# Layer 0 of a two-layer graph network: where the adjacency bits come from, when score pieces are filled, and which engines split q and k

## The chip, the cores and the metric

One core of a Trainium2 chip runs the whole program. The metric is the device time of one execution in microseconds, as the median over several runs. The engines are TensorE (PE, matrix products into PSUM), VectorE (DVE), ScalarE (ACT), GpSimd (POOL) and SyncE (SP), which here only issues DMA transfers. Each engine works through its own queue in order. [...]

## The reference

3327 rows of 128 features, an adjacency matrix of zeros and ones, and two layers. Layer 0 is cosine attention over the neighbours with a residual and a layer norm. Layer 1 is eight-head attention whose q, k and v are reshaped in an unusual way, with the adjacency added twice to the scores.

```python
def _L0_gnn_ref(x, adj, beta):
    norm2 = jnp.linalg.norm(x, axis=1, keepdims=True)
    cos = beta[0] * (x @ x.T) / (norm2 @ norm2.T + 1e-07)
    masked = cos + (1.0 - adj) * -1000000000.0
    P = jax.nn.softmax(masked, axis=1)
    return P @ x

def _L1_gnn_ref(x, spatial_encoding, edge_encoding, Wq, Wk, Wv, Wo):
    ...
    q = (x @ Wq.T).reshape(d, n, h)
    k = (x @ Wk.T).reshape(d, n, h)
    v = (x @ Wv.T).reshape(d, n, h)
    a = jnp.einsum('dnh,dmh->dnm', q, k) * scale
    a = a + spatial_encoding + edge_encoding
    a = jax.nn.softmax(a, axis=2)
    out = jnp.einsum('dnm,dmh->dnh', a, v)
    out = out.reshape(n, h * d)
    return out @ Wo.T

x = _layernorm(x + _L0_gnn_ref(x, adj, L0_gnn_beta), axis=-1)
x = _layernorm(x + _L1_gnn_ref(x, adj, adj, Wq, Wk, Wv, Wo), axis=-1)
```

## The kernel before

The rows are cut into 26 tiles of 128 (N = 3327 is padded to 3328). Layer 0 is a software pipeline written out by hand: the outer loop `for t in range(-2, T + 3)` makes one round for each tile, and the inner loop takes eight steps `k`. In one round the stages of five tiles are interleaved:

- tile t+3: `load` fetches the adjacency rows as fp32 (the buffer `raw`, which shows as `kn` in the profile; three such buffers), at step 5. `load_bits` fetches the same rows for tile t+4 once more through POOL's queue, converted to bf16 on the way (`bits`, two buffers).
- tile t+2: `adj_chunk` multiplies strided columns of `bits` by a unit matrix on PE (L396), which turns them, and ACT copies them as bf16 to `aT` (L397, one buffer); after seven chunks `aT` is written to DRAM for layer 1 (L399).
- tile t+1: the inverse of the norm products, by a logarithm and exponentials on ACT (L410, L417) and Newton steps on DVE (L424, L431), and `mask`, which turns `raw` into an additive mask in place (L403).
- tile t: `scores`. Four pieces of 832 columns; for each, `score_piece` makes two fp32 products on PE (L359) into a two-bank buffer `sc` (two buffers), and DVE scales (L441) and masks them and takes the running minimum (L444).
- tile t-1: `weights` (the exponentials, L460), `turn_weights` (transposes on PE, L134, copied to SBUF by DVE or ACT, L474 and L472) and `weigh0` (the product with x, L482).
- tile t-2: the layer norm (`norm_begin`, `norm_root`, `norm_end`) and `project_turn`, the transposed x1.
- tile t-3: `project`. Six products of 512 columns (L533) with the three weight matrices into the PSUM tile `pq`, which has one buffer: k = 0 and 1 make q, 2 and 3 make k, 4 and 5 make v. For q and k, ACT copies the product to SBUF (`row`, L549; q with its scale), POOL rounds it to `high` (L554) and subtracts to get `low` (L555), and SP writes both to DRAM (L558). For v, ACT copies to `nine` (L535) and SP writes it (L539).

Within one engine the order is the order of the code (a manual schedule for PE, ACT, DVE and POOL); the order on SP is chosen by a scheduler. In rounds from tile 8 on, `gather` rearranges q and k in DRAM for layer 1; its transfers have no fixed place on SP's queue and appear in many rounds.

Rounds 26 to 28 have no new tile. They finish the last three tiles while `first_max` already searches the maxima for layer 1, using the same `sc` buffers.

Layer 1 follows and takes the rest of the time. Its per-step order on PE, ACT, DVE and POOL is written out as well.

Of the kernel before, what the change touches and what calls it, by code (L numbers as in the profile page):

```python
# [45 lines left out]
def gnn_two_layers(  # L46
# [297 lines left out]
    with ExitStack() as l0:  # L344
        big = l0.enter_context(tc.tile_pool(name="l0_big", bufs=1))
        adj_raw = l0.enter_context(tc.tile_pool(name="adj_raw", bufs=2))
# [21 lines left out]
        tiles = [Tile0() for _ in range(T)]  # L368
        half = NP // 2
# [12 lines left out]
        def load_bits(t: int):  # L382

            u = tiles[t]
            u.bits = adj_raw.tile([P, NP], BF16, name="bits", bufs=2)
            load_adj(u.bits, nc.gpsimd, t)

        def adj_chunk(t: int, c: int):

            u = tiles[t]  # L390
            if c == 0:
                u.aT = ptp.tile([P, T, P], BF16, name="aT", bufs=1)
            a, b = 4 * c, min(4 * c + 4, T)
            tp = ps_tp.tile([P, 4, P], F32, name="tp")
            for k in range(a, b):
                nc.tensor.matmul(tp[:, k - a], every(u.bits, k), unit, start=True, stop=True)  # L396
            nc.scalar.copy(u.aT[:, a:b, :], tp[:, : b - a])  # L397
            if c == NCH - 1:
                nc.sync.dma_start(aT_s[t], u.aT.rearrange("p t k -> p (t k)"))  # L399
# [34 lines left out]

        def scores(t: int, j: int):
            u = tiles[t]
            if j == 0:
                u.s = work.tile([P, NP], F32, name="s")
                u.mn = small.tile([P, NPC], F32, name="mn")
            sc = score_piece(xT[:, t * P : (t + 1) * P], xT, j)  # L440
            nc.vector.scalar_tensor_tensor(  # L441
                piece(u.s, j), sc, by_q[:, t : t + 1], piece(u.y, j), op0=ALU.mult, op1=ALU.mult
            )
            nc.vector.tensor_tensor_reduce(  # L444
                out=piece(u.s, j),
                in0=piece(u.s, j),
                in1=piece(u.raw, j),
                scale=-1.0,
                scalar=BIG if j == 0 else u.mn[:, j - 1 : j],
                op0=ALU.add,  # L450
                op1=ALU.min,
                accum_out=u.mn[:, j : j + 1],
            )
# [73 lines left out]
        def project(t: int, k: int):  # L527
# [5 lines left out]
            nc.tensor.matmul(pq, u.x1T, ws[n][:, cols], start=True, stop=True)  # L533
            if n == 2:
                nc.scalar.copy(  # L535
                    nine[:, i * 64 : (i + 1) * 64, :H], pq.rearrange("p (s h) -> p s h", h=H)
                )
                if i == 1:
                    nc.sync.dma_start(  # L539
                        bass.AP(  # L540
                            tensor=v_s.tensor,
                            offset=v_s.offset + t * P * P * R9,
                            ap=[[P * R9, P], [1, P * R9]],
                        ),
                        nine.rearrange("p s r -> p (s r)"),
                    )
                return
            row = ptp.tile([P, 512], F32, name="row", bufs=2)
            nc.scalar.activation(  # L549
                row, pq, AF.Copy, scale=float(D) ** -0.5 if n == 0 else 1.0  # L550
            )
            high = ptp.tile([P, 512], F32R, name="high")
            low = ptp.tile([P, 512], F32R, name="low")
            nc.gpsimd.tensor_copy(high, row)  # L554
            nc.gpsimd.tensor_tensor(low, row, high.bitcast(F32), ALU.subtract)  # L555
            dst = (qn_s, kn_s)[n]
            for c, part in enumerate((high, low)):
# [9 lines left out]
        with tc.manual_schedule(  # L567
# [23 lines left out]
            for t in range(2):  # L591
                load_bits(t)
            nine = big.tile([P, P, R9], F32, name="nine")
            nc.gpsimd.memset(nine[:, :, H], 1.0)
# [31 lines left out]
            for i in range(2):  # L626
                nc.gpsimd.tensor_copy(
                    ws[i].rearrange("p (h s) -> p h s", h=H),
                    given[i].rearrange("p (s h) -> p h s", h=H),
                )  # L630

            k_first = 0
            for t in range(-2, T + 3):

                def there(n: int):
                    return 0 <= n < T

                for k in range(8):
                    if k == 0:
                        if there(t - 1):  # L640
                            weights(t - 1, 0)
                        if there(t - 3):
# [3 lines left out]
                        if there(t):  # L646
                            scores(t, 0)
# [3 lines left out]
                        if there(t - 3):  # L651
                            project(t - 3, 1)
                        if there(t - 2):
                            norm_root(t - 2)
                        if t >= T:
                            first_max(k_first)
                            k_first += 1
                        continue
                    if there(t) and k < NPC:
                        scores(t, k)  # L660
# [16 lines left out]
                    if k < 5 and there(t - 3):  # L677
                        project(t - 3, k + 1)
                    if k == 5 and there(t - 2):
                        project_turn(t - 2)  # L680
                    if there(t + 2):
# [14 lines left out]
                if there(t + 4) and t + 4 > 1:  # L696
                    load_bits(t + 4)
# [347 lines left out]
```

## Time and profile before

| what | value |
| --- | --- |
| median of 3 runs | 15358.9 us (15358.85 to 15360.56) |
| profiled execution | 15361.3 us, span 15359.5 us |
| PE, DVE, ACT, POOL busy over the span | 99%, 90%, 83%, 90% |
| granted TensorE clock, mean | 0.995 |
| start of layer 0 until the regular rounds | 0 to 121.8 us |
| regular rounds of tiles 3 to 23 | 121.8 to 668.9 us |
| rounds of tiles 24 and 25, drain, hand-over to layer 1 | 668.9 to 831 us |

How to read the lines shown further on. A row of the view by stretches gives the stretch, its length, then for PE, PE's weight loads, DVE, ACT and POOL the busy time with the number of instructions, then the granted clock, the mean busy share of the DMA engines and GB/s. A row of the timeline gives the start, the length, the engine, the line, the operation, the tiles written and read, the shapes and the count; in square brackets stands how long the engine was idle before it and what released it. A row of the waits gives who waited for whom, the total in us, the number of times and the longest. A matmul in fp32 shows as two records.

### The profile page before, as it was taken

Reading aid. Unit: us, or ns where it says so; the run is one execution under the profiler, and the core shown is the slowest. Engines: PE = TensorE matmul, PEld = TensorE weight load, DVE = VectorE, ACT = ScalarE, POOL = GpSimd, SP = SyncE. Lnnn points to the kernel's source line nnn. Section 1 sums busy time; section 2 is a strip of 40 time slices with the busy share of each in tenths; the row PEclk is TensorE's granted clock in tenths of the full one; section 3 lists DMA queues with packets and bytes.
Section 4 is the critical chain, followed back from the end, with each engine's and each line's share of the span. In section 5 each row is a group of like instructions: output and inputs, shape, how many; then the busy total and the mean of one; then the engine's idle time right before and its main releaser. Section 6 shows DMA issues by size and latency. Waiting matters only on the chain.

```text
span 15359.5 us, 494776 instructions
## 1 busy us (share of the span) xinstructions
PE 15192.6 (99%) x210460; PEld 6695.5 (44%) x210460; DVE 13818.7 (90%) x15851; ACT 12755.2 (83%) x25413; POOL 13765.0 (90%) x8979
## 2 busy tenths in 40 slices
PE   8899999999999999999999999999999999999999
PEld 5534444444444444444444444444444444444555
DVE  7889999999999999999999999999999999998776
ACT  7689998888888888888888888888888888888777
POOL 3389999999999999999999999999999999998887
PEclk9999999999999999999999999999999999999999
DMA  7732221111111111111111111111111111111112
GB/s 229 226 103 97 101 98 60 48 51 48 56 50 47 52 53 53 46 53 46 60 47 53 47 58 48 51 48 55 51 46 53 46 59 46 53 46 62 62 59 83
DMA packets 553135, 1018.81 MB, mean 66 GB/s; under 512 B 148711, under 2 KB 493284, under 8 KB 504582
## 3 DMA queue, kind: packets, MB, share of 16 engines
q1 hardware_dynamic: 547126, 965.00, 19.1%
q0 software_dynamic: 3792, 22.15, 0.8%
q8 instruction: 1648, 27.00, 0.7%
q14 instruction: 569, 4.66, 0.1%
HBM read 871.04 MB, written 192.54 MB: 69 GB/s over the span
## 4 chain that ended last, share of the span: by engine, by line
PE 96%; DMA 1%; DVE 1%; ACT 1%; issue 0%; SPq 0%; POOL 0%; DVEq 0%; ACTq 0%; POOLq 0%
PE acc L808 30%; PE ea L778 22%; PE m L262 16%; PE eb L791 13%; PE ea L791 10%; PE ea L797 1%; PE ea L764 1%; DMA aT_s<-aT 1%; PE eb L797 1%; PE acc L482 0%; PE pq L533 0%; PE sc L359 0%; ACT aT L397 0%; PE pp L993 0%; DMA qn_s<-high 0%
## 5 line engine op out<-in xcount | busy, mean ns | idle before, releaser
L899 POOL TENSOR_TENSOR pb<-pb,eT 128x768 f32<-128x768 f32 (+1 forms) x7488 | 13175.3, 1767 | 980.4 <-ACT pb L898 594.0
L277 DVE TENSOR_REDUCE mx<-m 128x2 f32<-128x1024 f32 x6753 | 8275.0, 1225 | 958.6 <-PE eb L797 555.4
L898 ACT ACTIVATE pb<-eb 128x768 f32<-128x768 f32 (+1 forms) x7488 | 5898.0, 788 | 2255.7 <-PE eb L797 1731.1
L262 PE MATMUL m<-kn,qx 32*128 32x512 f32 (+1 forms) x23128 | 6804.0, 471 | 0.1
L922 ACT ACTIVATE pa<-ea 128x384 f32<-128x384 f32 (+1 forms) x14976 | 6338.9, 478 | 23.0 <-PE ea L778 8.4
L808 PE MATMUL acc<-pb,vt 128*9 128x384 f32 (+1 forms) x29952 | 5903.7, 474 | 0.1
L808 PE MATMUL acc<-pa,vt 128*9 128x384 f32 (+1 forms) x29952 | 5903.7, 474 | 0.0
L298 DVE TENSOR_REDUCE mx<-m 128x1 f32<-128x512 f32 x6371 | 4338.5, 681 | 252.0 <-PE m L262 232.3
L791 PEld LDWEIGHTS <-one 3*128 3x128 bf16 x29952 | 1465.8, 91 | 5659.0 <-issue 4661.4
L778 PE MATMUL ea<-aT,two 128*32 128x384 bf16 (+1 forms) x59904 | 3715.6, 325 | 0.0
L797 PE MATMUL eb<-qx,kn 32*128 32x384 f32 (+1 forms) x13312 | 3030.2, 451 | 0.0
L797 PE MATMUL ea<-qx,kn 32*128 32x384 f32 (+1 forms) x13312 | 2938.7, 433 | 0.0
L262 PEld LDWEIGHTS m<-kn,qx 32*128 32x128 f32 x23128 | 2797.6, 182 | 216.3 <-DVE mx L298 4.7
L791 PE MATMUL ea<-cx,one 3*128 3x384 bf16 (+1 forms) x14976 | 2724.4, 324 | 0.2
L791 PE MATMUL eb<-cx,one 3*128 3x384 bf16 (+1 forms) x14976 | 2466.1, 326 | 16.9 <-ACT cx L869 16.7
L808 PEld LDWEIGHTS acc<-pa,vt 128*9 128x9 f32 x29952 | 1418.2, 91 | 399.9
L808 PEld LDWEIGHTS acc<-pb,vt 128*9 128x9 f32 x29952 | 1418.6, 91 | 387.0 <-issue 0.7
L778 PEld LDWEIGHTS <-two 128*32 128x32 bf16 x59904 | 938.1, 94 | 1421.5 <-issue 1231.0
L797 PEld LDWEIGHTS eb<-qx,kn 32*128 32x128 f32 x13312 | 1275.0, 188 | 0.0
L797 PEld LDWEIGHTS ea<-qx,kn 32*128 32x128 f32 x13312 | 1237.0, 182 | 8.0 <-issue 1.3
L302 DVE TENSOR_REDUCE mx<-m 128x2 f32<-128x512 f32 x1084 | 739.7, 682 | 20.3 <-PE m L262 19.1
L554 POOL CAST high<-row 128x512 fp32r<-128x512 f32 x104 | 96.0, 923 | 328.7 <-DMA qn_s<-high 209.9
(134 smaller groups left out, 5972.2 us busy)
## 6 DMA issues: line engine op xcount, KB each, us to landing
kn<-kp_s SPq DMA_DIRECT2D x512, 832.0 KB
vt<-v_s SPq DMA_DIRECT2D x288, 409.5 KB
kn<-kq_s SPq DMA_DIRECT2D x64, 832.0 KB
qx<-qp_s SPq DMA_DIRECT2D x1016, 48.0 KB
kn<-in_adj_dram SPq DMA_DIRECT2D x25, 1663.5 KB
qp_s<-qn_s SPq DMA_DIRECT2D x64, 416.0 KB
kp_s<-kx SPq DMA_DIRECT2D x32, 832.0 KB
kq_s<-kn_s SPq DMA_DIRECT2D x64, 415.9 KB
```

What stands on the lines that cost most here:

```text
L262: nc.tensor.matmul(dst, u.qx[rows(a), q * P : (q + 1) * P], u.km[rows(a), k0:k1], start=True, stop=True,)
L277: nc.vector.tensor_reduce(u.mx[:, h, qs[0], c], m, axis=AX.X, op=ALU.max)
L298: nc.vector.tensor_reduce(u.mx[:, a, qs[0], c : c + 1], m, axis=AX.X, op=ALU.max)
L302: nc.vector.tensor_reduce(u.mx[:, a, qs[0] : qs[1] + 1, c], m.rearrange("p (q k) -> p q k", q=2), axis=AX.X, op=ALU.max,)
L764: nc.tensor.matmul(dst[r], parts[u.i % 2][:, q, h], unit, start=start, stop=True, tile_position=(0, 32 * h), skip_group_check=True,)
L778: nc.tensor.matmul(e[r, : u.nq], two[:, r], aT[:, j, : u.nq], start=False, stop=True, tile_position=(0, 32 * c), skip_group_check=True,)
L791: nc.tensor.matmul(e[:, : u.nq], one[r], u.cx[r, : u.nq], start=True, stop=False, skip_group_check=True)
L797: nc.tensor.matmul(e[:, : u.nq], u.kx[rows(a), j * P : (j + 1) * P], u.qx[rows(a), : u.nq], start=False, stop=stop, skip_group_check=True,)
L808: nc.tensor.matmul(acc[32 * h : 32 * h + H + 1, : u.nq], u.vt[:, h, j], pts[h][:, : u.nq], start=(j == 0), stop=(j == T - 1), tile_positio ...
L898: nc.scalar.activation(pt_b[:, :, : u.nq], e_b[:, :, : u.nq], AF.Exp)
L899: nc.gpsimd.tensor_tensor(pt_b[:, :, : u.nq], pt_b[:, :, : u.nq], eT[:, j, : u.nq].unsqueeze(1).to_broadcast([P, 2, u.nq]), ALU.mult,)
L922: nc.scalar.activation(pt_a[:, h, : u.nq], e[:, : u.nq], AF.Exp)
```

## The change

Layer 1 isn't touched. In layer 0:

1. `load_bits` and its buffers go. `adj_chunk` reads the upper 16 bits of each fp32 word of `raw` as bf16 (`upper`), before `mask` overwrites `raw`. `aT` gets two buffers.
2. The score product leaves `scores` and becomes `fill`. The pieces 2 and 3 of tile t are filled at the ends of steps 0 and 1, the pieces 0 and 1 of tile t+1 at the ends of steps 6 and 7 of the round before.
3. `project` no longer makes `row`. ACT copies `pq` to `high`; in `project_rest` PE adds `less` (minus the unit matrix) times `high` to `pq` in PSUM, and ACT copies the remainder to `low`. POOL has no part in it. The scale of q moves into the weights, once at the start. `project` moves from the end of a step to the start of the next, and `project_turn` from step 5 to step 6. `nine` gets two buffers.

```diff
-        def load_bits(t: int):
...
+        def upper(t: int, k: int):
+
+            halves = tiles[t].raw.bitcast(BF16)
+            return halves.rearrange("r (p t h) -> r t h p", t=T, h=2)[:, k, 1, :]
...
-                u.aT = ptp.tile([P, T, P], BF16, name="aT", bufs=1)
+                u.aT = ptp.tile([P, T, P], BF16, name="aT", bufs=2)
...
-                nc.tensor.matmul(tp[:, k - a], every(u.bits, k), unit, start=True, stop=True)
+                nc.tensor.matmul(tp[:, k - a], upper(t, k), unit, start=True, stop=True)
...
+        def fill(t: int, j: int):
+            if there(t):
+                tiles[t].sc[j] = score_piece(xT[:, t * P : (t + 1) * P], xT, j)
...
-            sc = score_piece(xT[:, t * P : (t + 1) * P], xT, j)
+            sc = u.sc.pop(j)
...
-            nc.tensor.matmul(pq, u.x1T, ws[n][:, cols], start=True, stop=True)
+            nc.tensor.matmul(pq, u.x1T, ws[n][:, cols], start=True, stop=n == 2, skip_group_check=True)
...
-            row = ptp.tile([P, 512], F32, name="row", bufs=2)
-            nc.scalar.activation(
-                row, pq, AF.Copy, scale=float(D) ** -0.5 if n == 0 else 1.0
-            )
-            high = ptp.tile([P, 512], F32R, name="high")
+            u.pq = pq
+            u.high = ptp.tile([P, 512], F32R, name="high")
+            nc.scalar.copy(u.high, pq)
+
+        def project_rest(t: int, k: int):
+
+            u = tiles[t]
+            n, i = divmod(k, 2)
             low = ptp.tile([P, 512], F32R, name="low")
-            nc.gpsimd.tensor_copy(high, row)
-            nc.gpsimd.tensor_tensor(low, row, high.bitcast(F32), ALU.subtract)
+            nc.tensor.matmul(
+                u.pq, less, u.high, start=False, stop=True, skip_group_check=True
+            )
+            nc.scalar.copy(low, u.pq)
...
-            nine = big.tile([P, P, R9], F32, name="nine")
-            nc.gpsimd.memset(nine[:, :, H], 1.0)
+            nines = [big.tile([P, P, R9], F32, name=f"nine{i}") for i in range(2)]
...
-            for i in range(2):
-                nc.gpsimd.tensor_copy(
+            for i, by in enumerate((float(D) ** -0.5, 1.0)):
+                nc.gpsimd.tensor_scalar(
...
+            less = big.tile([P, P], F32R, name="less")
+            nc.vector.tensor_scalar_mul(less, ident, -1.0)
...
                     if k == 0:
                         if there(t - 1):
                             weights(t - 1, 0)
+                        if there(t):
+                            scores(t, 0)
                         if there(t - 3):
                             project(t - 3, 0)
                         if there(t - 2):
                             norm_begin(t - 2)
-                        if there(t):
-                            scores(t, 0)
                         if there(t - 1):
                             turn_weights(t - 1, 0)
                             weights(t - 1, 1)
-                        if there(t - 3):
-                            project(t - 3, 1)
                         if there(t - 2):
                             norm_root(t - 2)
+                        fill(t, 2)
+                        if there(t - 3):
+                            project_rest(t - 3, 0)
...
+                    if there(t - 3) and k < 6:
+                        project(t - 3, k)
...
-                    if k < 5 and there(t - 3):
-                        project(t - 3, k + 1)
-                    if k == 5 and there(t - 2):
+                    if k == 1:
+                        fill(t, 3)
+                    if k < 4 and there(t - 3):
+                        project_rest(t - 3, k)
+                    if k == 6 and there(t - 2):
                         project_turn(t - 2)
+                    if k >= 6:
+                        fill(t + 1, k - 6)
...
-                if there(t + 4) and t + 4 > 1:
-                    load_bits(t + 4)
```

More of the change, by code (lines that the diff above doesn't have):

```diff
@@ L345, in gnn_two_layers @@
         big = l0.enter_context(tc.tile_pool(name="l0_big", bufs=1))
-        adj_raw = l0.enter_context(tc.tile_pool(name="adj_raw", bufs=2))
         work = l0.enter_context(tc.tile_pool(name="l0_work", bufs=2))
@@ L368, in gnn_two_layers, with there @@
         tiles = [Tile0() for _ in range(T)]
+        for u in tiles:
+            u.sc = {}
+        def there(n: int):
+            return 0 <= n < T
         half = NP // 2
@@ L380, in load @@
                 nc.sync.dma_start(u.xr[:LAST], rows_of(x, t, D, LAST))
-        def load_bits(t: int):
-            u = tiles[t]
-            u.bits = adj_raw.tile([P, NP], BF16, name="bits", bufs=2)
-            load_adj(u.bits, nc.gpsimd, t)
+        def upper(t: int, k: int):
+            halves = tiles[t].raw.bitcast(BF16)
+            return halves.rearrange("r (p t h) -> r t h p", t=T, h=2)[:, k, 1, :]
         def adj_chunk(t: int, c: int):
@@ L532, in project @@
             pq = ps_x.tile([P, 512], F32, name="pq")
-            nc.tensor.matmul(pq, u.x1T, ws[n][:, cols], start=True, stop=True)
+            nc.tensor.matmul(pq, u.x1T, ws[n][:, cols], start=True, stop=n == 2, skip_group_check=True)
             if n == 2:
+                nine = nines[t % 2]
                 nc.scalar.copy(
@@ L547, in project @@
                 return
-            row = ptp.tile([P, 512], F32, name="row", bufs=2)
-            nc.scalar.activation(
-                row, pq, AF.Copy, scale=float(D) ** -0.5 if n == 0 else 1.0
-            )
-            high = ptp.tile([P, 512], F32R, name="high")
-            low = ptp.tile([P, 512], F32R, name="low")
-            nc.gpsimd.tensor_copy(high, row)
-            nc.gpsimd.tensor_tensor(low, row, high.bitcast(F32), ALU.subtract)
+            u.pq = pq
[4 more added lines that the diff above has]
+            n, i = divmod(k, 2)
+            low = ptp.tile([P, 512], F32R, name="low")
+            nc.tensor.matmul(
+                u.pq, less, u.high, start=False, stop=True, skip_group_check=True
+            )
+            nc.scalar.copy(low, u.pq)
             dst = (qn_s, kn_s)[n]
-            for c, part in enumerate((high, low)):
+            for c, part in enumerate((u.high, low)):
                 nc.sync.dma_start(
@@ L590, in gnn_two_layers @@
                 load(t)
-            for t in range(2):
-                load_bits(t)
-            nine = big.tile([P, P, R9], F32, name="nine")
-            nc.gpsimd.memset(nine[:, :, H], 1.0)
+            nines = [big.tile([P, P, R9], F32, name=f"nine{i}") for i in range(2)]
+            for nine in nines:
+                nc.gpsimd.memset(nine[:, :, H], 1.0)
             given = one_n.tile([P, NP], F32, name="n")
@@ L625, in gnn_two_layers @@
             nc.scalar.preload_act_table_set("natural_log_exp_and_others")
-            for i in range(2):
-                nc.gpsimd.tensor_copy(
+            for i, by in enumerate((float(D) ** -0.5, 1.0)):
+                nc.gpsimd.tensor_scalar(
                     ws[i].rearrange("p (h s) -> p h s", h=H),
                     given[i].rearrange("p (s h) -> p h s", h=H),
-                )
+                    by,
+                    None,
+                    op0=ALU.mult,
+                )
+            less = big.tile([P, P], F32R, name="less")
+            nc.vector.tensor_scalar_mul(less, ident, -1.0)
             k_first = 0
             for t in range(-2, T + 3):
-                def there(n: int):
-                    return 0 <= n < T
                 for k in range(8):
```

## The prediction

> **What bounds the kernel now.** The diff touches the first layer only, so I read the busy times by stretch first, to see how much of the span that is and which engine is full there. The twenty-one regular rounds (one row tile each, from tile 3 to tile 23) fill 121.8 to 668.9 us; what follows up to 831 us is the drain.
>
> ```profile
> 147.20:172.30 25.10, 22.76 (x135) 15.87 (x134) 23.11 (x32) 20.57 (x27) 9.40 (x11) 1.00 0.85 251
> 506.00:536.20 30.20, 25.03 (x135) 16.84 (x134) 21.28 (x29) 20.56 (x28) 14.08 (x14) 0.89 0.81 246
> 121.80:668.90 547.10, 494.08 (x2795) 343.62 (x2794) 468.40 (x653) 426.89 (x548) 222.41 (x228) 0.97 0.82 245
> ```
>
> The columns are length, then busy time of PE, weight loads, DVE, ACT and POOL, then granted clock, DMA share and GB/s. The first row is a clean round: 25.1 us, with PE at 22.8, DVE at 23.1, ACT at 20.6 and the DMA engines at 85%. The second is a round that lost 5 us to transfers, with no more work on any engine. The third gives the mean, 547.1 / 21 = 26.05 us, so about one microsecond of each round is transfer trouble (21 x 0.95 = 20 us in all). The other 14.5 ms run the same code before and after.
>
> No engine is full, so the round is set by waits. The waits of the same stretch, and ACT's instructions in the clean round in order of time:
>
> ```profile
> DVE s L441 <- PE sc L359: 50.6, 38, 6.8
> ACT row L549 <- PE pq L533: 35.9, 36, 1.6
> ACT nine L535 <- PE pq L533: 27.0, 20, 1.6
> ACT aT L397 <- PE tp L396: 20.2, 23, 1.8
> ```
> ```profile
> 147.25 1.70 ACT L460 ACTIVATE s<-s,mn 128x1664 f32<-128x1664 f32 x1
> 148.83 0.20 ACT L460 ACTIVATION_READ_ACCUMULATOR s<-s,mn 128x1 f32 x1
> 148.92 0.60 ACT L549 ACTIVATE row<-pq 128x512 f32<-128x512 f32 x1
> 149.40 1.69 ACT L460 ACTIVATE s<-s,mn 128x1664 f32<-128x1664 f32 x1
> ...
> 151.06 0.60 ACT L549 ACTIVATE row<-pq 128x512 f32<-128x512 f32 x1
> ...
> 151.90 3.06 ACT L410 ACTIVATE y<-norm_k,norm_c 128x3328 f32<-128x3328 f32 x1
> 155.21 0.60 ACT L549 ACTIVATE row<-pq 128x512 f32<-128x512 f32 x1 [0.26 <-PE pq L533]
> 155.70 1.59 ACT L417 ACTIVATE y<-y 128x1664 f32<-128x1664 f32 x1
> 158.80 0.60 ACT L549 ACTIVATE row<-pq 128x512 f32<-128x512 f32 x1 [1.51 <-PE pq L533]
> 159.29 1.58 ACT L417 ACTIVATE y<-y 128x1664 f32<-128x1664 f32 x1
> 162.33 0.59 ACT L535 COPY nine<-pq 128x512 f32<-128x512 f32 x1 [1.45 <-PE pq L533]
> 162.81 3.07 ACT L403 ACTIVATE kn<-kn,minus 128x3328 f32<-128x3328 f32 x1
> ```
>
> The reader is to see two things. From the first exponential (147.25) to the first copy of v (162.33) is 15.1 us, and the rest of the round, up to the next exponential at 172.34, is 10.0. And between any two reads of the bank pq (L549, L549, L549, L549, L535) stands an exponential, a logarithm or another long function: while ACT does that, PE fills pq again, so ACT hardly waits (3.2 us in the round, all because PE's steps are full: scores, turn, weighing and projection from 154.95 to 158.54 and again to 162.13 are 3.59 us without a gap).
>
> **The split of q and k: this sets the forecast.** pq has one buffer. Before, row frees it and POOL splits off the path. After, pq(k) is read by ACT (high), reduced by PE (minus high), and read by ACT again (low); only then may PE write pq(k+1). In the changed kernel's order low(k) is followed on ACT at once by high(k+1) (after k=3 by the first copy of v), with nothing between them. So four times a round ACT waits for a projection that can't start before ACT's own last instruction ends. The drain of the trace before has just that pair, two rows with nothing between:
>
> ```profile
> 739.31 0.60 ACT L549 ACTIVATE row<-pq 128x512 f32<-128x512 f32 x1 [4.50 <-PE pq L533]
> 741.18 0.60 ACT L549 ACTIVATE row<-pq 128x512 f32<-128x512 f32 x1 [1.27 <-PE pq L533]
> ```
>
> 1.27 us idle at full clock. ACT's pace, start to start: exponential 1.67, copy of 512 columns 0.48, logarithm 3.05, each L417 1.57, the two small ones 0.36 together. First part of the round: exponentials 3.34, high 4 x 0.48 = 1.92, low 4 x 0.48 = 1.92, small 0.36, logarithm 3.05, L417 3.14: 13.73. Waits 4 x 1.27 = 5.08. Sum 18.8 us against 15.1: +3.7 a round.
>
> Is the subtraction itself late? It isn't in the trace; the nearest row, the 128x512 fp32r product of L262, took 0.50 us alone, and three on different rows of the array started within 0.01 us, so 0.17 to 0.50; as a plain fp32 product it would be L533's 0.86. For k=2 and 3 it follows turn 0.43 and weighing 0.90, and low stands behind L417 1.57: 1.33 + 0.50 is just hidden, at 0.86 it costs 0.2. For k=1 a logarithm covers it. For k=0 PE has turn, a score piece of 1.40 and the subtraction after the exponential, ACT 2.3 us until low: even to late by 0.3. I take 0 of it; upper end 1 us a round. Behind a late low stand on ACT high, the logarithm and all that follows; DVE waits for those.
>
> **Score pieces filled early.** The 50.6 us that DVE waited for scores go, 2.4 us a round. But DVE isn't last in the new order. The same eight products (2 x 1.40 = 2.8 us) are moved from steps 2 and 3 to steps 6 and 7, where PE must also feed ACT's aT copies. PE's queue there, from the first v projection: projection 1.05, turn 0.43, weighing 0.9, adjacency 0.4, projection 0.9, turn 0.4, weighing 0.9; wait for mask and first aT copy until 5.35; then 0.35, wait for pt until 6.3, 0.35, wait for aT until 6.85, turn 0.2, weighing 0.9, x1 0.25, fill 1.4 (to 9.6), adjacency 0.7, weighing 0.45, fill 1.4 (to 12.15), adjacency 0.5; the last aT copy ends at 13.4. From nine that is 12.2 us; the same count without the fills gives 9.4 where the trace shows 10.0. I take 12.2 - 10.0 = +2.2; bounds 0 (fills fall wholly into PE's gaps) and +2.8.
>
> **Upper halves of the words.** POOL's 26 loads (8.4 to 14.5 us each to land) go; these took 18.1 of 82 points of the DMA share. adj_chunk now reads raw, one round earlier than mask did. The load (1663.5 KB) is issued some 13 us into a round and first read in the next round's step 4, some 36 us later; at the 251 GB/s of the clean row it takes 7 us alone and under 20 behind everything else, so no wait. The matmuls (26 x 0.23) and weight loads stay. Two aT and two nine buffers end ACT's waits of 9.9 and 9.4 us. On SP the load of raw is now issued between kn high and low, waiting for DVE's last scores; three splits stand behind it and all have 8 us until their buffer is needed. high's own buffers: high(k+2) follows high(k) by 8.5 to 9.5 us; in the clean round before POOL got that buffer 7.5 us after the issue (150.22 to 157.76), so I take no wait; if a gather stands in front, some us in eight rounds, 0 to 20. The 20 us of transfer trouble vanish in a longer round; my 31.0 has none of it.
>
> **POOL's high and low** (104 x 0.92 and 104 x 1.53) leave. L444 ran 1.08 us alone and up to 2.19 beside them; DVE gains some 0.8 us a round, but it has 23 us of work in 31, so this is worth nothing here. Scaling the weights in the copies of L627 (2.04 us each) and making the matrix less happen once, 80 us before their first use. POOL's memset of raw's pad now waits for PE and ACT too; only the next load stands behind it.
>
> **The sum.** A round is 18.8 + 12.2 = 31.0 us; twenty-one make 651 against 547.1: +104. Tile 24's round has no adjacency, and gets 3.7 and about half of the fills: +5. Tile 25's round and the drain: each of twelve splits holds PE by about a copy, 0.6 us, partly in gaps: +6. Start: two adjacency loads gone while x and the raw tiles load (0 to 20 us, DMA busy 0.76 to 0.91), and earlier scores for tiles 0 to 2: -8, bounds 0 and -15. Sum +107: the profiled span 15359.5 becomes 15466; the median of the runs is 15358.9, so the same number stands against it.
>
> [...] The granted clock fell to 0.50 from 746.0 to 783.5 us although PE's longest gap in the 3.4 us before was 1.72 us. In the new round PE idles up to 1.6 us at the start of a round and about 0.6 to 1.4 four times more. If that row's pattern holds, a slow stretch of 3.4 us a round costs up to 1.5 us: +30 in all; I keep this for the upper end. [...]
>
> **Rivals.** (a) The fills fall into PE's gaps: a round of 18.8 + 9.7 = 28.5; 21 x 2.45 = +51, with the other terms +54: 15414. For it: PE was idle 2.3 us of the clean round; against: those gaps lie before the fills. (b) More is lost: clock or DMA-held high buffers on top, +40 to +60: 15515. (c) Faster: low and the projection behind it are hidden and the round becomes PE's own. PE's least work is scores 5.6, turns 2.8, weighing 5.9, projections 5.2, adjacency 2.2, x1 0.2, subtractions 1.2 = 23.1; with 1.3 for the start of a round 24.4: 21 x (24.4 - 26.05) = -35, with the start -8: 15316. It wins only if the round falls below 26 us, that is if ACT waits under 0.1 us instead of 1.27 at each of the four places; the single buffer of pq speaks against it. (d) Nothing measurable: DMA gains just pay for a milder chain, 15359.
>
> **Chances.** Forecast 0.66, (a) 0.14, (b) 0.08, (c) 0.08, (d) 0.04. A change of 0.2% (31 us) is about what can be told from none. (a) is above that. Faster 0.08, same 0.05 (with the lowest edge of a), slower 0.87. The forecast's own range is 15430 to 15500 (fills 0.6 to 2.8, subtraction 0 to 1 us a round, gathers); with most of (a) 15395 to 15505.
>
> **What would show it.** Right: ACT waits of about 1.3 us on the projection before three of the four highs and before nine in every round; rounds of 30 to 32 us; 18 to 19.5 us from first exponential to nine and 11.5 to 12.5 after it; no wait of DVE for scores; DMA share in the rounds near 0.55; POOL nearly empty. Wrong: rounds near 25 (the pair of low and high isn't exposed), near 28.5 (fills hidden), or ACT's high waiting for DMA.

## The result and the profile after

The changed kernel took **15472.1 us** (median of 4 runs, 15470.78 to 15474.7) against 15359.6 us of the kernel before on the same chip: 1.0075 times the time, 95% interval 1.0063 to 1.0087. The prediction was 15466. The profiled execution spans 15469.9 us, 110.4 more than the 15359.5 of before.

Layer 1 from its first exponential on took 14535.4 us against 14536.9, so the whole loss lies in layer 0 and in the hand-over. Below, a round lasts from one tile's first exponential to the next tile's, its first part ends where the first copy of v begins, and the hand-over lasts from the last tile's first exponential to layer 1's first.

| | before | after | difference | forecast |
| --- | --- | --- | --- | --- |
| start, until tile 3's round | 121.8 | 117.7 | -4.1 | -8 |
| 21 rounds, tiles 3 to 23 | 547.1 | 641.7 | +94.6 | +104 |
| round of tile 24 | 20.8 | 24.8 | +4.0 | +5 |
| round of tile 25 and hand-over | 132.8 | 150.3 | +17.5 | +6 |
| layer 1 | 14536.9 | 14535.4 | -1.5 | 0 |

The busy times by stretch of the changed kernel, one round and then all twenty-one (length, busy time of PE, weight loads, DVE, ACT and POOL, granted clock, DMA share, GB/s), answer to the rows of 25.10 and 547.10 us:

```profile
392.70:423.20 30.50, 23.97 (x138) 16.16 (x137) 21.29 (x32) 22.27 (x31) 0.10 (x1) 1.00 0.58 192
117.70:759.40 641.70, 504.79 (x2878) 339.83 (x2877) 448.71 (x653) 468.80 (x632) 2.12 (x21) 1.00 0.57 189
```

All twenty-one rounds are 30.5 or 30.6 us; there is no disturbed one like that of 30.2 us before, and the clock stays at 1.00. No engine comes near 30.5 us of work: PE is busy 24.0, ACT 22.3. What fills the rest is in the view of waits, from 120 to 780 us:

```profile
POOL kn L94 <- DVE mn L452: 604.6, 20, 30.5
DVE pt L482 <- PE tp L134: 148.7, 110, 2.3
PEld pq L541 <- ACT low L569: 125.8, 88, 1.7
...
ACT high L559 <- PE pq L541: 80.2, 66, 1.2
...
ACT aT L401 <- PE tp L400: 56.7, 42, 1.4
...
ACT nine L544 <- PE pq L541: 26.7, 22, 1.2
```

Two engines wait for each other. PE's projection (L541) waits for ACT's low copy (L569), four times a round; ACT's next read of pq, high (L559) or nine (L544), waits for that projection, 88 times in all at 1.21 us. The first row is POOL waiting a whole round to clear a pad: nothing but the next load stands behind it. ACT's queue in one round, in order of time, shows the pairs:

```profile
394.33 0.58 ACT L559 CAST high<-pq 128x512 fp32r<-128x512 f32 x1
394.80 1.70 ACT L468 ACTIVATE s<-s,mn 128x1664 f32<-128x1664 f32 x1
...
396.82 0.58 ACT L569 CAST low<-pq 128x512 fp32r<-128x512 f32 x1
398.62 0.59 ACT L559 CAST high<-pq 128x512 fp32r<-128x512 f32 x1 [1.22 <-PE pq L541]
399.10 3.07 ACT L414 ACTIVATE y<-norm_k,norm_c 128x3328 f32<-128x3328 f32 x1
402.07 0.58 ACT L569 CAST low<-pq 128x512 fp32r<-128x512 f32 x1
403.86 0.59 ACT L559 CAST high<-pq 128x512 fp32r<-128x512 f32 x1 [1.22 <-PE pq L541]
...
405.83 0.58 ACT L569 CAST low<-pq 128x512 fp32r<-128x512 f32 x1
407.63 0.59 ACT L559 CAST high<-pq 128x512 fp32r<-128x512 f32 x1 [1.22 <-PE pq L541]
...
409.60 0.58 ACT L569 CAST low<-pq 128x512 fp32r<-128x512 f32 x1
411.39 0.59 ACT L544 COPY nine<-pq 128x512 f32<-128x512 f32 x1 [1.21 <-PE pq L541]
```

Every low is followed by a read of the next projection with 1.22 us of idleness before it. No low has a bracket: the subtraction on PE is always done by then. From 392.65 (the first exponential) to 411.39 is 18.7 us, and 11.8 remain until 423.20. The subtraction as PE ran it, from the groups of instructions with shapes kept apart (busy, mean ns of one, idle before):

```profile
L566 PE MATMUL pq<-high,less 128*128 128x512 f32 x84 | 50.2, 597 | 0.0
```

### The profile page after: what moved, and what is told of

It is laid out like the page before. It is cut to its first block, busy times and chain, and to the rows that moved or that the text cites. A ratio compares the mean times of both kernels' runs of the same rounds, so it can differ in the third digit from the quotient of the medians.

```text
span 15469.9 us, 494707 instructions
## 1 busy us (share of the span) xinstructions
PE 15209.2 (98%) x210564; PEld 6680.7 (43%) x210564; DVE 13794.7 (89%) x15852; ACT 12819.8 (83%) x25517; POOL 13511.5 (87%) x8718
## 3 DMA queue, kind: packets, MB, share of 16 engines
q1 hardware_dynamic: 547126, 965.00, 19.1%
## 4 chain that ended last, share of the span: by engine, by line
PE 93%; ACT 0%; issue 0%; DMA 0%; POOL 0%; DVE 0%; SPq 0%; ACTq 0%; DVEq 0%; POOLq 0%
PE acc L827 30%; PE ea L797 21%; PE m L262 16%; PE eb L810 13%; PE ea L810 10%; PE ea L816 1%; PE ea L783 1%; PE eb L816 1%; PE pp L1012 0%; DMA orow<-o_s 0%; ACT pa L941 0%; ACT oT L1009 0%; PE otp L1008 0%; POOL orow L1001 0%; ACT pb L917 0%
## 5 line engine op out<-in xcount | busy, mean ns | idle before, releaser
L277 DVE TENSOR_REDUCE mx<-m 128x2 f32<-128x1024 f32 x6753 | 8275.4, 1225 | 966.2 <-PE eb L816 538.6
L262 PE MATMUL m<-kn,qx 32*128 32x512 f32 (+1 forms) x23128 | 6793.1, 470 | 0.2 <-DVE mx L302 0.2
L941 ACT ACTIVATE pa<-ea 128x384 f32<-128x384 f32 (+1 forms) x14976 | 6335.6, 478 | 25.1 <-PE ea L797 11.3
L262 PEld LDWEIGHTS m<-kn,qx 32*128 32x128 f32 x23128 | 2794.0, 181 | 222.4 <-DVE mx L298 4.3
```

What stands on the lines that cost most here:

```text
L262: nc.tensor.matmul(dst, u.qx[rows(a), q * P : (q + 1) * P], u.km[rows(a), k0:k1], start=True, stop=True,)
L277: nc.vector.tensor_reduce(u.mx[:, h, qs[0], c], m, axis=AX.X, op=ALU.max)
L941: nc.scalar.activation(pt_a[:, h, : u.nq], e[:, : u.nq], AF.Exp)
```

## Experiments

Three edits make the change: the split on ScalarE and TensorE, the upper halves, the early score products. Four versions each undo one part or two; then the order on ScalarE, the buffers of pq, and the hand-over were changed. All ratios are to the kernel before, timed on the same chip; the intervals are 95%. That kernel's own median was 15355.8 to 15362.8 us in the five timings behind the table, so a difference of a few us between two rows of it shows nothing. In the split spread, the first copy of v itself stands later, so its two parts don't compare with the others.

| version | start | 21 rounds | a steady round, its two parts | hand-over | median |
| --- | --- | --- | --- | --- | --- |
| before | 121.8 | 547.1 | 25.1 = 15.1 + 10.0 | 106.4 | 15359.6 |
| changed | 117.7 | 641.7 | 30.5 = 18.7 + 11.8 | 125.7 | 15472.1 |
| POOL's split | 119.1 | 522.8 | 25.2 = 12.8 + 12.4, later 24.6 | 111.1 | 15327.1 |
| the split alone | 121.6 | 649.4 | 30.7 = 21.6 + 9.1 | 126.1 | 15490.5 |
| upper halves alone | 115.4 | 518.2 | 24.0 = 14.7 + 9.3 | 111.2 | 15320.9 |
| products in place | 113.7 | 652.8 | 30.7 = 21.6 + 9.1 | 122.9 | 15483.8 |
| second load back | 125.3 | 648.2 | 30.6 = 18.7 + 11.8 | 126.0 | 15486.2 |
| low beside its high | 116.9 | 588.8 | 28.0 = 16.2 + 11.8 | 123.5 | 15412.0 |
| split spread | 117.7 | 642.7 | 30.7 = 26.5 + 4.2 | 127.1 | 15470.6 |
| pq from a ring of three | 111.4 | 531.6 | 25.2 = 13.8 + 11.4 | 122.6 | 15348.5 |

### POOL's split back

```diff
-            u.high = ptp.tile([P, 512], F32R, name="high")
-            nc.scalar.copy(u.high, pq)
...
-            nc.tensor.matmul(u.pq, less, u.high, start=False, stop=True, skip_group_check=True)
-            nc.scalar.copy(low, u.pq)
...
+            nc.scalar.copy(row, pq)
...
+            nc.gpsimd.tensor_copy(high, row)
+            nc.gpsimd.tensor_tensor(low, row, high.bitcast(F32), ALU.subtract)
```

> The changed kernel with the split of q and k put back on POOL (ACT copies pq to row, POOL makes high and low); upper halves, early fills and the new places of the projections stay. Theory (ACT's low is followed at once by a read of the next pq, and the one buffer of pq makes ACT wait 1.2 us for the projection, four times a round): no read of pq stands directly behind another, so the four waits of 1.2 and the four copies of 0.48 both go. The round falls from 30.6 to 24 to 25.5 us, the first part from 18.7 to some 13 us; in all 15320 to 15350. Rival (ACT simply has more work, the waits are slack that would be spent elsewhere): only 4 x 0.48 = 1.9 us a round are saved, the round is 28.7, in all about 15432.

Measured: 15327.13 us, ratio 0.9981 (0.9972 to 0.9991). The rounds by stretch:

```profile
119.10:641.90 522.80, 467.81 (x2794) 325.00 (x2793) 469.40 (x647) 429.28 (x548) 208.97 (x189) 1.00 0.69 225
```

One part undone turns a loss of 112 us into a gain of 29 (15355.8 for the kernel before, timed beside it). The rival is out: the loss is the split's. The first part is 12.8 us and not 15.1 because PE makes the products of two score pieces in the second part now: with POOL's split and products in place, in the next section, it is 14.7.

### The split alone, and the upper halves alone

The split alone puts the second load, one aT and one nine back and computes each score product just ahead of its reader. The upper halves alone have POOL's split and score products in place; the changed order of the projections stays in both.

```diff
-            sc = u.sc.pop(j)
+            sc = score_piece(xT[:, t * P : (t + 1) * P], xT, j)
...
-                        fill(t, 2)
```

> The changed kernel with the other two parts undone: the second load through POOL with one aT and one nine, and score products just ahead of their readers; the split alone is ScalarE's and TensorE's. Theory (the split carries the whole loss; loads cost a start of some 8 us and little in a slow round that leaves the transfers time; early products worth 0 to 10 us here): rounds 31 to 32 with a first part near 21.6, time 15485 to 15510. Rival (the loss needs the early products or the upper halves as well, by PE's fuller queue): 15470 or less.

> The changed kernel with two of its three parts undone: the split is on POOL (row, high, low) and each score product stands just ahead of the VectorE operation that reads it. What is left is the adjacency turned from the upper halves of the raw words, without the second load. Theory (the second load is worth the disturbed rounds and the start and nothing else, and with POOL's split the early score products shift 2.3 us from the first part of a round to the second): rounds all within 24.4 to 25.4, first part 15.1, second part about 10, hand-over near 110 us, time 15325 to 15345, so within 0.1% of the version with POOL's split and early score products. Rival (the gain of that version came from the early score products, the loads were hidden): rounds still scatter up to 30 us and the time is within 10 us of before, 15350 to 15365.

Measured: the split alone 15490.47 us, ratio 1.0087 (1.0071 to 1.0102), a steady round of 30.7 us; the upper halves alone 15320.9 us, ratio 0.9977 (0.9967 to 0.9986). The split's theory holds, with a round a little shorter than the 31 to 32 it gave. The split needs no help for its loss: 30.7 against 25.1 is **+5.6 us a round** by itself. For the upper halves both sides missed. The time lies below the theory's 15325 and far below the rival's 15350; a clean round is 24.0, not 25; but four of its rounds are still 25.2 to 29.9 us, the scatter that the rival named and the theory excluded. The waits of that version between 115 and 640 us say why:

```profile
POOL high L557 <- ACT row L554: 155.4, 54, 11.9
POOL high L557 <- DMA qn_s<-high: 114.5, 12, 19.1
```

POOL, which makes high, waited up to 19.1 us for the store of an earlier high to free its buffer; behind POOL stand row, and so ACT, and so the projection.

### Score products in place, and the second load back

Each undoes one other part of the changed kernel, ScalarE's and TensorE's split kept. Of the second load's edit, the line that reads it:

```diff
-                nc.tensor.matmul(tp[:, k - a], upper(t, k), unit, start=True, stop=True)
+                nc.tensor.matmul(tp[:, k - a], every(u.bits, k), unit, start=True, stop=True)
```

> The changed kernel with every score product made again just ahead of DVE's use of it; split on ACT and PE and upper halves stay. Theory (the second part of the round, 11.8 us, is PE's queue with two fills in it, but taking them out puts 1.4 us between projection and subtraction in steps 2 and 3, where only 2.05 us of ACT's work cover 1.33 + 0.5 now): second part 9.8 to 10.3, first part 20.5 to 22, round 31 to 32, in all 15480 to 15520. Rival (the early fills cost their 1.8 us of the second part and nothing stands against it): round 28.7, in all about 15433.

> The changed kernel with the adjacency loaded once more as bf16 through POOL's queue, and one buffer each of aT and nine as before; split on ACT and PE and early fills stay. Theory (at 30.6 us a round transfers are hidden anyway): the DMA share of the rounds rises from 0.57 to about 0.73, the round stays within 0.5 us of 30.6, the start gets some 4 us longer, in all 15470 to 15490. Rival (the second load still costs what it cost before, about 1 us a round and more beside gathers): 15495 or more.

Measured: products in place 15483.83 us, ratio 1.0083 (1.0068 to 1.0098); second load back 15486.22 us, ratio 1.0083 (1.0067 to 1.01). Both times lie in the theories' ranges and neither rival's came. In detail the theories missed: the second part is 9.1 us and not 9.8 to 10.3, and the start 7.6 us longer and not some 4. Early products take 2.9 us from the first part (21.6 to 18.7), add 2.7 to the second (9.1 to 11.8) and leave a steady round within 0.2 us of where it was. The loads cost 7.6 us at the start and one round of 35.7 us, and nothing in a round of 30.6.

### Low beside its high

The same instructions; the low copy now comes straight after its high, and the long function stands between it and the next high.

```diff
                             turn_weights(t - 1, 0)
+                        if there(t - 3):
+                            project_rest(t - 3, 0)
+                        if there(t - 1):
                             weights(t - 1, 1)
...
-                        if there(t - 3):
-                            project_rest(t - 3, 0)
...
```

> The changed kernel with low moved on ACT directly behind high, so that the long function of the step stands between low and the next high. The same instructions on every engine. Theory (what costs is the direct neighbourhood of two dependent reads; between high and low lies only the subtraction, 0.5 to 0.7 us with the semaphores, instead of the projection's 1.22): the first part falls from 18.7 to about 16.6, the round to 28.5, in all 15415 to 15445. Rival (ACT's amount of work sets the round): no change, 15472.

Measured: 15412.01 us, ratio 1.0037 (1.0024 to 1.005), slightly better than expected. ACT's queue has the other order, and half the wait:

```profile
407.24 0.57 ACT L559 CAST high<-pq 128x512 fp32r<-128x512 f32 x1
408.40 0.59 ACT L569 CAST low<-pq 128x512 fp32r<-128x512 f32 x1 [0.59 <-PE pq L566]
408.88 1.59 ACT L421 ACTIVATE y<-y 128x1664 f32<-128x1664 f32 x1
410.37 0.58 ACT L559 CAST high<-pq 128x512 fp32r<-128x512 f32 x1
```

A subtraction's round trip costs 0.59 us, a projection's 1.22. Four times the difference is 2.5 us, and the round fell from 30.56 to 28.04, by 2.5. So the round is paid wait for wait. That the subtraction's trip is the shorter fits with its one record where a projection has two, but wasn't measured by itself.

### The split spread over the whole round

Again the same instructions. Projection, high copy, subtraction and low copy were set into the queues so that a long ACT function stands between any two reads of pq where the round has one, up to the copies of v in its last steps.

```diff
...
+                        elif k == 2:
+                            project_rest(t - 3, 1)
+                            project(t - 3, 2)
+                        elif k == 3:
+                            project_out(t - 3, 2)
+                            project_less(t - 3)
...
```

> The changed kernel with the same instructions in another order: each projection, its high copy, its subtraction and its low copy are put into the queues so that at least one long ScalarE function stands between any two ScalarE reads of the one pq buffer, over the whole round and not its first part only. Theory (the loss is the four round trips of 1.22 us that ScalarE waits for pq, and the first part being filled with low copies): ScalarE's waits on the projection fall from 4.9 us a round to under 1.5, rounds 25.5 to 28, time 15355 to 15420; TensorE's own work (about 22.3 us a round with POOL's split, and four subtractions of 0.7) sets the lower end. Rival (the loss is the added work of ScalarE and TensorE itself, wherever it stands): rounds 29 or more, 15435 to 15475.

Measured: 15470.58 us, ratio 1.0073 (1.006 to 1.0087). **The theory fell by its number**: ACT's waits on the projection and the subtraction did go, to 1.4 us a round, and the time stayed. The waits of this version between 120 and 780 us (here L541 is the projection, L578 low, L531 the turn of x1, L550 nine):

```profile
DVE pt L482 <- PE tp L134: 165.5, 44, 5.7
ACT aT L401 <- PE tp L400: 138.2, 84, 2.5
PEld pq L541 <- ACT low L578: 50.4, 66, 1.2
...
PEld pq L531 <- ACT nine L550: 30.4, 21, 1.5
...
ACT low L578 <- PE pq L569: 29.3, 21, 1.5
```

The waits moved. PE stands in its queue until ACT has read pq, and the transposes behind it come late: ACT's waits for aT rose from 56.7 to 138.2 us and DVE's for pt from 148.7 to 165.5, the longest of them from 2.3 to 5.7. In addition the clock fell to half for 3.4 us in twenty of the 21 rounds, which the last section takes up; the one round without it, tile 3's, took 29.2 us and not 30.3 to 30.7, so up to 1.5 us of each round may be the clock's. So ACT's order alone didn't end the loss. The rival's range holds the time, but the rival, the added work itself, isn't proved by this. The next version decides.

### Projections from a ring of three

All instructions keep their places. The bank of pq goes to the ring of the transposes, which gets three buffers, and projections, and the turn of x1, take theirs from it.

```diff
-        ps_tp = l0.enter_context(tc.tile_pool(name="l0_tp", bufs=2, space=PSUM))
+        ps_tp = l0.enter_context(tc.tile_pool(name="l0_tp", bufs=3, space=PSUM))
...
-            pq = ps_x.tile([P, 512], F32, name="pq")
+            pq = ps_tp.tile([P, 4, P], F32, name="tp").rearrange("p a b -> p (a b)")
```

> The changed kernel with its projections taken from the ring of the transposes, which gets the bank that pq had and so three buffers in place of two; the order of all instructions is kept. A projection may then be computed while ScalarE has yet to read the difference of the one before. Theory (the round is longer because a low copy and the next high copy stand side by side on ScalarE and one buffer forces a round trip through TensorE between them): the four waits of 1.22 us go, the first part falls from 18.7 to about 14 us, rounds 25.5 to 27.5, time 15365 to 15410. Rival (the wait only moves to TensorE's queue, as in the spread order, where the rounds stayed at 30.6): rounds 29.5 or more, 15450 to 15475.

Measured: 15348.46 us, ratio 0.9991 (0.9981 to 1.0), better than the theory's range and hardly to be told from the kernel before. The same two copies side by side on ACT, without the wait (pq now shows as tp), and the rounds:

```profile
399.70 0.57 ACT L569 CAST low<-tp 128x512 fp32r<-128x512 f32 x1
400.17 0.60 ACT L559 CAST high<-tp 128x512 fp32r<-128x512 f32 x1
400.64 1.61 ACT L421 ACTIVATE y<-y 128x1664 f32<-128x1664 f32 x1
402.14 0.59 ACT L569 CAST low<-tp 128x512 fp32r<-128x512 f32 x1
```
```profile
111.40:643.00 531.60, 482.50 (x2878) 343.41 (x2877) 444.15 (x658) 459.76 (x631) 2.12 (x21) 1.00 0.69 227
```

The round is 25.2 us: the first part lost 4.9, which is 4 x 1.22, and the second 0.4. The added copies and subtractions are still all there, so their work is not the loss. **It is the one buffer of pq, which made every low, next projection and next high a chain.** The transposes share the third buffer, which wasn't tried by itself; the 4 x 1.22 us and the same sum with low beside its high tie the loss to the projections. The range was missed because it left out tiles 24 and 25 (4.9 and 3.5 us shorter) and the start (6.3 us earlier), and the second part gave 0.4 us too.

### The hand-over

POOL makes high and low for the last three tiles alone.

```diff
+            if t > T - 4:
...
+                nc.gpsimd.tensor_copy(u.high, u.row)
+                nc.gpsimd.tensor_tensor(low, u.row, u.high.bitcast(F32), ALU.subtract)
+            else:
+                nc.tensor.matmul(u.pq, less, u.high, start=False, stop=True, skip_group_check=True)
+                nc.scalar.copy(low, u.pq)
```

> The changed kernel with POOL's split (row, high, low) for the last three tiles alone, whose q and k are made after the last round. Theory (the 19 us that the hand-over to layer 1 grew are the projection and the subtraction that stand in TensorE's queue ahead of layer 1's first row maxima): from the end of the weights of the last tile to layer 1's first exponential 108 to 114 us in place of 125.7, time 15455 to 15463, rounds unchanged at 30.5. Rival (the growth is TensorE's half clock there, which the split doesn't set): 122 us or more and a time of 15468 to 15476.

Measured: 15456.8 us, ratio 1.0064 (1.005 to 1.0078). The hand-over, from the last tile's first exponential as in the table, is 110.0 us, so 15.7 of the 19.3 us by which it grew belong to the split; where the other 3.6 went was not found. The rival's half clock is there in both. The slow stretch of the hand-over, first in the changed kernel, then with POOL's split in it:

```profile
837.20:934.50 97.30, 57.35 (x137) 21.51 (x136) 48.07 (x61) 23.90 (x49) 7.59 (x8) 0.50 0.37 106
```
```profile
838.00:920.20 82.20, 47.18 (x121) 18.02 (x121) 44.45 (x52) 18.02 (x38) 18.82 (x20) 0.50 0.39 108
```

PE has 10.2 us more to do there at half clock. The timeline of the changed kernel shows how it falls into the row maxima's way (L262 makes the scores, L277 takes the maximum):

```profile
878.89 2.08 PE L541 MATMUL pq<-wq,x1T 128*128 128x512 f32 x2
...
881.64 0.79 PE L566 MATMUL pq<-high,less 128*128 128x512 f32 x1 [0.68 <-ACT high L559]
...
882.36 0.80 PE L262 MATMUL sc<-kn 32*128 32x512 f32 x3
882.47 0.59 ACT L569 CAST low<-pq 128x512 fp32r<-128x512 f32 x1 [0.88 <-PE pq L566]
...
883.11 2.08 PE L541 MATMUL pq<-wq,x1T 128*128 128x512 f32 x2
883.20 1.23 DVE L277 TENSOR_REDUCE mx<-sc 128x2 f32<-128x1024 f32 x1 [2.97 <-PE sc L262]
```

From the projection to the scores PE passes the subtraction and waits 0.68 us for high ahead of it; DVE meanwhile idles 2.97 us.

### Towards a faster kernel

Three versions combine what paid. The first is the upper halves alone with four buffers each for high and low and one aT:

```diff
-            high = ptp.tile([P, 512], F32R, name="high")
+            high = ptp.tile([P, 512], F32R, name="high", bufs=4)
```

> The version with upper halves alone (POOL's split, no early score products) with four buffers each for high and low in place of two, and one aT in place of two to make room. Theory (its rounds of 25 to 30 us are POOL waiting up to 19.1 us for the stores of high, which then holds row and the projection): all rounds at 23.9 to 24.3, 21 rounds 502 to 508 in place of 518.2, time 15303 to 15313. Rival (the stores are late because the queue is, and more buffers only move the wait to aT, nine or x1): 15317 or more.

> The fastest version so far (upper halves, POOL's split, score products in place, four buffers each for high and low) with projections taken from the ring of three. Theory (what is left of ScalarE's waits in a round is 1.6 us for the second copy of v and some 0.7 us for row, both on the one pq): 0.5 to 1.5 us a round less, 22.5 to 23.5, time 15280 to 15302. Rival (TensorE, over 95% busy in these rounds, is the bound and the waits are its shadow): rounds 23.7 or more, 15305 to 15315.

> The changed kernel with three edits: projections from the ring of three, the last three tiles split on POOL, and score products just ahead of their readers; ScalarE's and TensorE's split stays in the 21 regular rounds, as do the upper halves. Theory (with the round trips gone the early score products hold up the turns behind them, as with POOL's split, where they cost 25.2 against 24.0 us a round; and the drain's price is the projection and subtraction ahead of the row maxima): rounds 23.7 to 24.7, hand-over 108 to 113 us, time 15300 to 15325. Rival (ScalarE, 1.9 us of low copies a round fuller, now bounds the round whatever TensorE's order): rounds 25.0 or more, 15333 or more.

Measured: with four buffers 15311.75 us, ratio 0.9966 (0.9954 to 0.9979), all 21 rounds at 24.0 us, so the late stores were the cause and didn't just move on. With the ring of three on top, **15297.45 us, ratio 0.9958 (0.9945 to 0.997)**, the fastest of all, rounds 23.0, four of them 25:

```profile
110.20:601.30 491.10, 470.30 (x2795) 326.20 (x2794) 457.46 (x652) 424.65 (x547) 193.29 (x189) 1.00 0.74 241
```

Without the ring PE showed 482.1 us busy of 503.5, and the rival took that for the floor; with it PE shows 470.3 of 491.1 for the same products, so it was no floor. The third version keeps ScalarE's and TensorE's split, with the ring, products in place and POOL in the hand-over: 15328.7 us, ratio 0.9979 (0.9969 to 0.9988), between the ranges of its theory and its rival. Its rounds alternate between 24.0 and 25.3 us; why they alternate was not found.

## Why the prediction was right, step by step

**The waits of the split.** Forecast: four times 1.27 us on ACT, before three highs and nine. Measured: 1.22, at those places, in every round. First part 18.8 forecast, 18.7 measured. That these waits are the loss, and that the single buffer makes them, is shown by the ring: with three buffers they go, and the round shrinks with them, 30.56 to 25.2. That the loss doesn't depend on the added copies is shown by the same run.

**The subtraction.** Forecast hidden, 0.17 to 0.50 us or 0.86 long. Its records average 0.60, and it is hidden in the rounds: no low waits. In the hand-over it isn't (see there).

**Score products filled early.** The forecast of +2.2 us for the second part is what the time shows as a sum (11.8 against 10.0, +1.8), and DVE's waits inside the first part are gone. One of 1.7 us a round is new, ahead of the next tile's first piece, where DVE is early; "no wait of DVE for scores" was too much. But **as a price of this edit it was wrong**. With the split kept, products in place give the same steady round (30.7 against 30.5), and the split alone is +5.6 us, not +3.7. The forecast's 18.8 for the first part already had the gain of moving the products out in it, so the split was charged too little and the products too much, by some 2 us each. With POOL's split they do cost: 24.0 in place, 25.2 or 24.6 early.

**Upper halves.** No wait on the loads, DMA share 0.57 (forecast 0.55), no disturbed round: as forecast. In the long round the loads are worth nothing, as the second load put back shows (30.6). The step that they are worth only 20 us of trouble falls for a short round: with upper halves alone a clean round is 24.0, against 25.1. The order of the projections and the second nine are also changed there, and these weren't separated; a second aT is not needed for it, since the version with four buffers has one and 24.0 in every round. The start gave 4.1 us, not 8, though the loads are worth nearly all of the 8: without them, products in place both times, it falls from 121.6 to 113.7. The early products, which the forecast had as a help there, took 4.0 back (117.7).

**POOL.** Nearly empty, 2.1 us in 21 rounds, and worth nothing, as forecast: in the ring version POOL is as empty and its round of 25.2 is no shorter than with POOL's split.

**DMA.** No high waited for a store, as forecast; it happens in the shorter rounds of POOL's split, up to 19.1 us. It happened in the kernel before too, of which the prediction read one clean round. The wait there from 121.8 to 668.9 us:

```profile
POOL high L554 <- DMA qn_s<-high: 200.9, 18, 21.0
```

The six rounds of over 28 us each have such a wait of 15.1 to 21.0 us that ends in them; in no other round is one over 13.2. So what the prediction called transfer trouble looks like this wait rather than the second load: without the load and with two buffers such rounds remain, with four they are gone. The kernel before with four buffers alone wasn't run.

**The hand-over: the mis-sized term.** Forecast +6 for tile 25 and the drain, "each of twelve splits holds PE by about a copy, 0.6 us, partly in gaps"; measured +17.5. The rows from 878.89 show what the step left out. The clock there is half, and in PE's queue the subtraction, and before it a wait for high, stand ahead of the scores of layer 1's maxima. With POOL's split in these three tiles 15.7 us come back. Against it stand 9.4 us too many in the rounds (30.56 for 31.0), 1 in tile 24, 1.5 in layer 1 and 3.9 too few at the start: 11.5 - 9.4 - 1.0 - 1.5 + 3.9 = 3.5, the difference of 107 to 110.4. That the total came closer than its terms is luck: two of them were off by some 10 us in opposite ways.

**The row of the clock.** The 30 us kept for the upper end weren't needed: the rounds show 1.00 throughout, with PE gaps of up to 1.59 us. In the rounds of the kernel before, the clock fell seven times. Three of these, such as the one that gives 0.77 from 505 to 515 us, came after a PE gap of 3.5 to 4.2 us. The other four, like those of the spread order and of the hand-over, came with no gap over 2.2 us, so keeping PE's gaps short didn't by itself keep the clock.

**Rivals.** (a) Hidden fills, 28.5 us a round, fell: the fills lengthen the second part by 1.8 us, though as an edit they cost the round nothing. (b) Clock or late high buffers fell with rounds at full clock and no high that waits for a store. (c) PE's own round near 24.4 needed the four waits gone; the ring took them away and got 25.2 with these early products, 24.0 in every other round with products in place. Its condition was named rightly, and the single buffer spoke against it rightly. (d) fell.

## What to carry to other kernels

When work is taken off a side engine and put into the accumulator, count how often each engine must hand that one bank to another before it is free: each hand-over is a round trip between two queues, here 1.22 us for a projection and 0.59 for a subtraction, and it appeared wherever two uses of the bank stood next to each other. Reordering can move such a wait to the other queue without ending it, as in the split spread (rounds of 30.7 us against 30.5); another buffer for the same value ended it (25.2), and here a shared ring gave one without a bank more. A price is found by doing that part alone: two edits in one round can have a right sum and wrong shares.

## What the runs showed of the hardware

The clock fell without any long gap. In the spread order PE's longest wait between 120 and 780 us was 1.3 us, yet the clock was at half in part of twenty of the 21 rounds. Two neighbouring stretches of that version:

```profile
359.20:362.61 3.41, 1.46 (x3) 0.44 (x3) 0.00 (x0) 2.99 (x6) 0.00 (x0) 1.00 0.57 233
362.61:366.02 3.41, 3.20 (x9) 2.13 (x9) 1.95 (x3) 2.60 (x7) 0.00 (x0) 0.50 0.77 270
```

The slow stretch follows the sparse one, in which PE was busy for 1.46 us of 3.41. In three rounds, from 305.8 to 397.9 us, the mean clock is 0.67 from 331.4 to 336.5, from 362.1 to 367.2 and from 392.8 to 397.9 us and 1.00 in the rest: it fell once a round. In the kernel before, PE was busy for 0.09 to 1.65 us of the 3.41 us ahead of each of the seven falls in its rounds.

A sparse stretch alone didn't bring a fall. In the split alone one of the same length had PE busy for 0.71 us, less than in the row above, and the clock stayed at 1.00; two stretches that divide the sparse time between them (last two rows) show 2.58 and 1.53 us, at 1.00 too:

```profile
650.31:653.72 3.41, 0.71 (x4) 0.19 (x2) 2.85 (x9) 2.81 (x6) 0.00 (x0) 1.00 0.97 328
648.43:651.84 3.41, 2.58 (x9) 0.98 (x7) 2.56 (x6) 3.23 (x4) 0.15 (x1) 1.00 0.98 359
651.84:655.25 3.41, 1.53 (x4) 0.87 (x5) 1.39 (x5) 1.66 (x6) 0.00 (x0) 1.00 1.07 290
```

So in these runs neither PE's longest gap nor its busy time in one such stretch tells whether the clock falls; what decides it was not shown, and no run was made to test it. In the hand-over the changed kernel's clock fell at 837.2 us although PE was busy for at least 2.55 us (75%) of every stretch of that length from 826 us to 837.2 us, and it stayed at 0.50 until after 934 us. Many products there use 32 rows of the array (L262); whether that counts wasn't tested.
